# The skip mixing of a spectral layer, on images instead of transposed pixels

## The chip, the cores and the metric

The kernel runs on one core of a Trainium2 chip. The metric is device time in microseconds, lower is better. The engines are called as the profile calls them: PE (matmul), PEld (weight load), DVE (vector), ACT (scalar), POOL (GpSimd) and SP, which here only issues transfers.

## The reference, cut to what matters

Two layers work on an array of 4 x 32 images of 128 x 128 numbers, in float32. Layer 1 (a pairwise attention and a mixture of experts) is untouched. Layer 0 is a Fourier layer with attention over the 32 images of a set; for every set b:

```
x   = group norm of the input (32 groups of 4 of the last axis), then instance norm -> xn
k, q = spectral convolutions of xn at half size;  v = xn * Vsw + spectral_conv(xn)    (32 heads)
p_attn = softmax over the 32 images of (q . k)
av  = p_attn @ v
p   = av * Psw + spectral_conv(av, Pcw)        # summed over heads
a   = inorm(p + x);  then two more Fourier layers on inorm(a)
```

What passes through `v` and `p` by the skip weights alone needs no Fourier transform: it is a 32 x 32 mixing of the images of the set, the same for every pixel. That mixing (with the identity for `+ x`) is what the change is about: for each pixel, 32 numbers in, 32 numbers out, on the group-normed input.

## The kernel before

Layer 0 is a loop over b in 0..3, written in plain program order; a planner (the framework's list scheduler) orders each engine's instructions by their place in the program and by the time at which it expects them to be ready, so later work, loads above all, can be placed ahead of earlier work that is not ready. Layer 1 has its order written out by hand and follows.

The image set is held as `xt`: the rows (first pixel axis) on the 128 partitions, then 32 images, then 128 columns. The columns fall into 32 groups of 4 for the group norm; `image_sums` computes for each group the mean `gm` and the inverse deviation `gr`, and `by_group`, which holds `gr` and minus `gm * gr` of the 32 groups on all partitions.

Inside the loop over b, the part around the change runs so:

- From the attention probabilities `ph` the kernel makes `cp`, the 32 x 32 mixing, on four blocks of 32 partitions (`cm`, `cd`, lines 651 to 657), and from it the block matrix `bd` (line 659): 128 x 128, with the 32 x 32 mixing four times on the diagonal.
- `skips(c0)` treats 16 columns. It turns them so that four columns times 32 images lie on partitions and the rows on the free axis: 16 matmuls with the identity into `pxt` (line 671). Four ACT instructions norm and move them to `xq` (line 681), with the scale and bias of their group. Four matmuls with `bd` (line 690) give `sk`, with the rows on partitions again, and one ACT copy (line 693) puts them into `q`. Eight calls treat all 128 columns.
- The calls are spread over a loop that does the Fourier part: `for x0 in range(0, KX, NK)`, five passes over slices of the modes (13, 13, 13, 13 and 12 rows of 33 modes). In each pass four tiles `xb` are loaded from the DRAM tile `xd` (line 706, two transfers of 214.5 KB to a tile, four buffers), copied to PSUM as `xw` by ACT (line 715), and multiplied with the weights `gb`: 16 products `u` to a pass, six by POOL (line 721) and ten by DVE (line 723), in six buffers. Each `u` goes through PE with the probabilities `pr` (line 726), in matmuls with 32 output columns, and is summed in `po`, which ACT copies into `rs` at the end of the pass (line 736). Two calls of `skips` are made in each of the first four passes, after the tiles i = 1 and i = 3.
- After the passes, `py` (line 746) transforms `rs` back, and `add_p` (line 759, DVE) adds the result onto `q`, group of eight images by group. `q` is then used by all that follows in this b, and the output of the layer is stored to `x1` from `xr`, which is `xt` in place (line 919).

At the end of a b, `gl` (buffer tag `y`, one buffer) is scaled by ACT (line 902) and added to `xr` by POOL (line 909); the images of b+1 are loaded as `x` (line 122), from SP and ACT. In PSUM, tag `a` holds `po` and `pxt`, tag `b` holds `sk` (two buffers each).

Of the kernel before, what the change touches and what calls it, by code (L numbers as in the profile page):

```python
# [7 lines left out]
F32 = mybir.dt.float32  # L8
AF = mybir.ActivationFunctionType
ALU = mybir.AluOpType  # L10
# [3 lines left out]
P = 128  # L14
B, T, H, C = 4, 32, 128, 128
# [3 lines left out]
GI = 8  # L19
# [56 lines left out]
NK = 13  # L76
# [28 lines left out]
def layer0(  # L105
    tc, x, kq_modes, kq_mirror, vcw, pcw, m0cw, m1cw, mcol0, heads, heads_row, small_row, by_p, inv_cols, dram, x1, first
):
    nc = tc.nc
# [7 lines left out]
    const, ps, images, values, modes = (p.__enter__() for p in pools + right)  # L116
# [32 lines left out]
    ident = const.tile([P, P], F32, name="ident")  # L149
# [125 lines left out]
    def image_sums(b, xt):  # L275


        rows8 = ps.tile([64, 4, C], F32, name="rows8", tag="wide")
        for g in GROUPS:
            xx2 = grp.tile([P, GI, C], F32, name="xx2", tag="pr", bufs=6)  # L280
            nc.scalar.activation(xx2, xt[:, g : g + GI], AF.Square)
            for h in range(2):
                m = g // 4 + h
                for k, src in enumerate((xt[:, 4 * m : 4 * m + 4], xx2[:, 4 * h : 4 * h + 4])):
                    nc.tensor.matmul(
                        rows8[32 * k : 32 * k + 32],
                        one_of_8[:, 7 - m : 39 - m],
                        src,
                        start=m == 0,
                        stop=m == 7,  # L290
                    )
        ev = grp.tile([64, 4, C], F32, name="ev", tag="v", bufs=3)
        nc.scalar.copy(ev, rows8)
        s12 = ps.tile([P, 2, 512], F32, name="s12", tag="wide")[:, :, :T]
        for j in range(4):
            for k in range(2):
                r = slice(32 * k, 32 * k + 8)
                nc.tensor.matmul(s12[:, k, j::4], ev[r, j], ident[r, r], start=True, stop=True)
        sv = small.tile([P, 2, T], F32, name="sv", tag="pk_sq")
        nc.vector.tensor_copy(sv, s12)  # L300

        tot = one("tot", 2)
        nc.vector.tensor_reduce(tot, sv, AX.X, ALU.add)
        mg = sums("mg", group, tot)
        gm = one("gm")
        nc.vector.tensor_copy(gm, mg[:, 0:1])
        gv = one("gv")
        nc.vector.tensor_mul(gv, gm, gm)
        nc.vector.tensor_tensor(gv, mg[:, 1:2], gv, ALU.subtract)
        gr, _ = inv_std("gn_r", gv, 1)  # L310
        gs = one("gs")
        nc.vector.tensor_mul(gs, gm, gr)

        both = small.tile([P, 2, 32], F32, name="both", tag="both")
        nc.vector.tensor_scalar(both[:, 0], of_group, gr, None, ALU.mult)
        nc.vector.tensor_scalar(both[:, 1], of_group, gs, -1.0, ALU.mult, ALU.mult)
        by_group = small.tile([P, 2, 32], F32, name="by_group", tag="by_group")
        nc.vector.tensor_copy(by_group, sums("bg", ones, both))
        n = 1 + 2 * KY
        colg = small.tile([P, 2, n], F32, name="colg", tag="colg")  # L320
        nc.vector.tensor_scalar(colg[:, 0], cols1[:, :n], gr, None, ALU.mult)
        nc.vector.tensor_scalar(colg[:, 1], cols2[:, :n], gr, None, ALU.mult)
        m128 = one("m128")
        nc.vector.tensor_scalar(m128, gm, 128.0, None, ALU.mult)

        gs128 = one("gs128")
        nc.vector.tensor_scalar(gs128, gs, 128.0, None, ALU.mult)
        gg = one("gg")
        nc.vector.tensor_mul(gg, gs, gs128)
        gr2 = one("gr2")  # L330
        nc.vector.tensor_mul(gr2, gr, gr)
        grs = one("grs")
        nc.vector.tensor_scalar(grs, gs, gr, -2.0, ALU.mult, ALU.mult)
        y12 = small.tile([P, 2, T], F32, name="y12", tag="pk")
        nc.vector.tensor_scalar(y12[:, 0], sv[:, 0], gr, gs128, ALU.mult, ALU.subtract)
        nc.vector.tensor_scalar(y12[:, 1], sv[:, 1], gr2, gg, ALU.mult, ALU.add)
        nc.vector.scalar_tensor_tensor(
            y12[:, 1], sv[:, 0], grs, y12[:, 1], ALU.mult, ALU.add
        )
        nc.vector.tensor_scalar(y12, y12, 1.0 / NPIX, None, ALU.mult)  # L340
        my = sums("my", ones, y12)
        ym, yv = per_image("ym"), per_image("yv")
        nc.vector.tensor_copy(ym, my[:, 0])
        nc.vector.tensor_mul(yv, ym, ym)
        nc.vector.tensor_tensor(yv, my[:, 1], yv, ALU.subtract)
        yr, _ = inv_std("n1_r", yv)
        ysc = scalars(ALU.mult, "n1_s", yr, par[:, N1W : N1W + 1])
        return by_group, colg, m128, ysc
# [286 lines left out]
    for b in range(B):  # L635
# [27 lines left out]
            ALU.mult,  # L663
        )
        q = big.tile([P, T, C], F32, name=f"q_{b}", tag="q")

        def skips(c0):
            px = ps.tile([P, 4, P], F32, name="pxt", tag="a")
            for k in range(4):
                for j in range(4):  # L670
                    nc.tensor.matmul(
                        px[32 * j : 32 * j + 32, k],
                        xt[:, :, c0 + 4 * k + j],
                        ident,
                        start=True,
                        stop=True,
                    )
            xq = grp.tile([P, 4, P], F32, name="xq", tag="v", bufs=3)
            for k in range(4):
                g = c0 // 4 + k  # L680
                nc.scalar.activation(
                    xq[:, k],
                    px[:, k],
                    AF.Identity,
                    bias=by_group[:, 1, g : g + 1],
                    scale=by_group[:, 0, g : g + 1],
                )
            sk = ps.tile([P, 16, T], F32, name="sk", tag="b")
            for k in range(4):
                nc.tensor.matmul(  # L690
                    sk[:, 4 * k : 4 * k + 4], xq[:, k], bd, start=True, stop=True
                )
            nc.scalar.copy(q[:, :, c0 : c0 + 16], sk.rearrange("w c t -> w t c"))

        rs = big.tile([P, KX, KY], F32, name=f"rs_{b}", tag="rs")
        at_c = 0
        for x0 in range(0, KX, NK):
            nk = min(NK, KX - x0)  # L700
            m = nk * KY
            po = ps.tile([P, NK * KY], F32, name="po", tag="a")[:, :m]
            for i in range(4):
                xb = late.tile([P, 2, NK * KY], F32, name="xb", tag="xb")[:, :, :m]
                for r in range(2):
                    nc.sync.dma_start(
                        out=xb[:, r],
                        in_=xd[8 * i : 8 * i + 8, r, x0 : x0 + nk]
                        .rearrange("s x y -> s (x y)")
                        .unsqueeze(1)  # L710
                        .to_broadcast([8, 16, m]),
                    )
                xw = ps.tile([P, 2, 512], F32, name="xw", tag="wide")[:, :, :m]
                for r in range(2):
                    nc.scalar.copy(xw[:, r], xb[:, r])
                for k in range(2):
                    for ri in range(2):
                        u = grp.tile([P, 2, NK * KY], F32, name="u", tag="pr", bufs=6)[:, :, :m]
                        gk = gb[:, k, ri, x0 * KY : x0 * KY + m].unsqueeze(1).to_broadcast([P, 2, m])
                        if (2 * k + ri + 4 * i) % 8 in (1, 4, 6):  # L720
                            nc.gpsimd.tensor_tensor(u, xb, gk, ALU.mult)  # L721
                        else:
                            nc.vector.tensor_tensor(u, xw, gk, ALU.mult)  # L723
                        for r in range(2):
                            j = 2 * ri + r
                            nc.tensor.matmul(  # L726
                                po[32 * j : 32 * j + 32],
                                pr[:, i, k],
                                u[:, r],
                                start=i == 0 and k == 0,  # L730
                                stop=i == 3 and k == 1,
                            )
                if i % 2 and at_c < C:
                    skips(at_c)
                    at_c += 16
            nc.scalar.copy(rs[:, x0 : x0 + nk].rearrange("p x y -> p (x y)"), po)
        if b + 1 == B:
            for p in reversed(right):
                p.__exit__(None, None, None)
# [807 lines left out]
```

## Time and profile before

| what | value |
|---|---|
| time, three runs | 3195.37, 3197.76, 3202.53 us; median 3197.76 |
| span of the profiled execution, first to last instruction | 3194.2 us |
| PE busy | 2961.2 us (93%) |
| DVE, ACT, POOL busy | 2318.6, 2324.8, 2135.8 us |
| `skips` at work (first line 726 to last copy to `rs`), b = 0 to 3 | 108 to 177, 365 to 436, 633 to 702, 888 to 957 us |
| granted PE clock, mean | 0.967 |
| HBM read, written | 68.16, 20.00 MB |

The profiled execution has no time of its own beside its span in what is recorded; the span lies 3.6 us below the median of the runs. A row of a group of instructions reads: line, engine, operation, output <- inputs, shapes, number, busy time and mean duration of one. fp32 matmuls appear as two records each, and some records can be missing. In the rows of a window, the first number is its length, then the busy time of each engine with the number of its instructions, the granted PE clock, the mean busy share of the 16 DMA engines and the GB/s moved. In the rows of the chain of waits, the columns are start, duration and what ran.

### The profile page before, as it was taken

To read this page: it belongs to the slowest core of one execution; us is meant where nothing else is said; L and a number is where in the kernel's file an instruction comes from. 1 tells how busy PE (TensorE), PEld (TensorE's weight loads), DVE (VectorE), ACT (ScalarE), POOL (GpSimd) and SP (SyncE) were. 2 spreads that over 40 slices of the span, in tenths; PEclk is the share of its full clock that TensorE was granted. 3 is DMA by queue.
4 is the path that set the end of the run, shared out by engine and by line. 5 is a ranking of instruction groups with operands and counts; after the bars stand their busy time and mean duration, and the time that the engine had idled before them with its cause. 6 is when DMAs were issued, how large, how long until landed. Compare 5 with 4: busy or idle time off the path is not lost.

```text
span 3194.2 us, 53401 instructions
## 1 busy us (share of the span) xinstructions
PE 2961.2 (93%) x19698; PEld 1556.6 (49%) x19698; DVE 2318.6 (73%) x5072; ACT 2324.8 (73%) x3205; POOL 2135.8 (67%) x1879
## 2 busy tenths in 40 slices
PE   7899899899898889999999999998999999999997
PEld 4377367458558744443344443444444444444443
DVE  6766767768787466777666868866778776777887
ACT  2435344354343489998999999998999999999992
POOL 2621641561461289878788797889878889888773
PEclk8899999899998799999999999999999999999998
DMA  6301310230140211010111010011010011101000
GB/s 138 116 11 30 101 44 4 64 106 1 36 125 1 57 31 30 8 31 7 30 37 24 14 24 14 8 39 30 22 30 8 14 37 24 37 1 31 14 14 14
DMA packets 151925, 112.57 MB, mean 35 GB/s; under 512 B 36750, under 2 KB 140273, under 8 KB 151057
## 3 DMA queue, kind: packets, MB, share of 16 engines
q1 hardware_dynamic: 135825, 103.40, 12.2%
q10 hardware_dynamic: 15840, 5.77, 0.8%
q8 instruction: 156, 2.56, 0.3%
q14 instruction: 104, 0.85, 0.1%
HBM read 68.16 MB, written 20.00 MB: 28 GB/s over the span
## 4 chain that ended last, share of the span: by engine, by line
PE 56%; POOL 12%; ACT 9%; DVE 7%; issue 6%; DMA 0%; POOLq 0%; DVEq 0%; ACTq 0%; SPq 0%
PE d L1349 18%; PE po L1368 10%; PE px L1255 6%; ACT r L1399 4%; PE n L1349 3%; POOL e L1408 3%; POOL e L1407 3%; PE po L726 3%; PE four L261 2%; PE pv L256 2%; PE px L247 2%; PE px L246 2%; ACT e L1415 2%; POOL kx L1014 2%; DVE r L1404 2%
## 5 line engine op out<-in xcount | busy, mean ns | idle before, releaser
L1404 DVE TENSOR_TENSOR r<-n,r 128x1024 f32<-128x1024 f32 (+1 forms) x1056 | 961.8, 952 | 479.2 <-PE n L1349 398.5
L1407 POOL TENSOR_TENSOR e<-r 128x512 f32<-128x512 f32 x528 | 674.1, 1277 | 269.9 <-DVE r L1404 269.1
L1399 ACT ACTIVATE r<-d 128x1024 f32<-128x1024 f32 (+1 forms) x1056 | 793.4, 803 | 71.5 <-PE n L1349 57.8
L1411 ACT ACTIVATE r<-r 128x1536 f32<-128x1536 f32 x528 | 783.5, 1484 | 16.7
L1408 POOL TENSOR_TENSOR e<-e,r 128x512 f32<-128x512 f32 x528 | 672.1, 1273 | 41.4
L1349 PE MATMUL d<-qe,ke 32*128 32x512 f32 (+3 forms) x2304 | 606.7, 603 | 39.7 <-ACT r L1399 36.4
L1368 PE MATMUL po<-e,kx 128*128 128x512 f32 (+3 forms) x1152 | 594.4, 605 | 17.4 <-POOL e L1420 17.4
L1349 PE MATMUL n<-qe,ke 32*128 32x512 f32 (+3 forms) x2304 | 606.2, 601 | 0.0
L1349 PE MATMUL n<-qf,kf 32*128 32x512 f32 (+3 forms) x2304 | 552.3, 554 | 0.0
L1349 PE MATMUL d<-qf,kf 32*128 32x512 f32 (+3 forms) x2304 | 550.8, 554 | 0.0
L1259 DVE SCALAR_TENSOR_TENSOR xc<-px,wgt,xc 128x128 f32<-128x128 f32 x1024 | 358.3, 350 | 43.1 <-PE px L1255 10.6
L1415 ACT ACTIVATE e<-e 128x512 f32<-128x512 f32 x528 | 325.8, 617 | 67.2 <-POOL e L1408 66.2
L1368 PEld LDWEIGHTS po<-e,kx 128*128 128x128 f32 x1152 | 175.4, 188 | 393.7 <-issue 307.7
L1349 PEld LDWEIGHTS d<-qe,ke 32*128 32x128 f32 x2304 | 176.9, 184 | 359.5 <-ACT r L1399 340.1
L721 POOL TENSOR_TENSOR u<-xb,gb 128x858 f32<-128x858 f32 (+1 forms) x120 | 233.1, 1969 | 126.7 <-PE po L726 108.3
L1349 PEld LDWEIGHTS d<-qf,kf 32*128 32x128 f32 x2304 | 220.5, 186 | 176.9 <-issue 164.2
L811 POOL TENSOR_TENSOR spec<-spec,part 128x264 f32<-128x264 f32 x64 | 55.4, 865 | 336.6 <-DVE part L808 174.8
L1255 PE MATMUL px<-we,x2t 128*128 128x512 f32 x512 | 265.8, 605 | 6.9 <-DVE xc L1259 5.8
L723 DVE TENSOR_TENSOR u<-xw,gb 128x858 f32<-128x858 f32 (+1 forms) x200 | 206.5, 1085 | 51.4 <-PE po L726 34.3
L1349 PEld LDWEIGHTS n<-qf,kf 32*128 32x128 f32 x2304 | 228.0, 185 | 18.6 <-issue 11.2
L726 PE MATMUL po<-u,pr 128*32 128x429 f32 (+1 forms) x1280 | 187.5, 537 | 20.5 <-POOL u L721 8.7
L1349 PEld LDWEIGHTS n<-qe,ke 32*128 32x128 f32 x2304 | 177.8, 183 | 9.3 <-DVE r L1404 0.9
(360 smaller groups left out, 4184.3 us busy)
## 6 DMA issues: line engine op xcount, KB each, us to landing
xb<-xd SPq DMA_DIRECT2D x128, 214.5 KB
xc<-x SPq DMA_DIRECT2D x29, 512.0 KB
x<-x SPq DMA_DIRECT2D x16, 512.0 KB
qf<-qe SPq DMA_DIRECT2D x64, 128.0 KB
out<-xc SPq DMA_DIRECT2D x15, 512.0 KB
xb<-xd SPq DMA_DIRECT2D x32, 198.0 KB
gb<-gd SPq DMA_DIRECT2D x4, 1056.0 KB
x<-in_x SPq DMA_DIRECT2D x8, 512.0 KB
```

The source lines that it names most:

```text
L721: nc.gpsimd.tensor_tensor(u, xb, gk, ALU.mult)
L726: nc.tensor.matmul(po[32 * j : 32 * j + 32], pr[:, i, k], u[:, r], start=i == 0 and k == 0, stop=i == 3 and k == 1,)
L1255: nc.tensor.matmul(px, x2t[:, k * P : (k + 1) * P], we[:, e0 : e0 + 4], start=True, stop=True)
L1259: nc.vector.scalar_tensor_tensor(xc[:, k], px[:, e], wgt[:, k, e0 + e : e0 + e + 1], xc[:, k], ALU.mult, ALU.add)
L1349: nc.tensor.matmul(o, k, q, start=turn == 0 or g > 0, stop=turn == 1 or g > 0)
L1368: nc.tensor.matmul(sums[c, h][:, q0 : q0 + c1 - c0], kx[:, jb], e[:, c0:c1], start=jb == 0, stop=is_last and q0 > 2 * P, skip_group_check= ...
L1399: nc.scalar.activation(r[:, g], d, AF.Ln, scale=1.0 / DSCALE)
L1404: nc.vector.tensor_tensor(r[:, g], part, r[:, g], ALU.mult)
L1407: nc.gpsimd.tensor_tensor(e, r[:, 1], r[:, 2], ALU.add)
L1408: nc.gpsimd.tensor_tensor(e, e, r[:, 0], ALU.add)
L1411: nc.scalar.activation(r, r, AF.Exp, scale=-1.0)
L1415: nc.scalar.activation(e, e, AF.Exp)
```

## The change

The mixing works on a second copy of the images in which a partition is (width piece j, image t): `xs`, 4 pieces x 32 images on partitions, 32 rows of pixels x 128 columns on the free axis. (The axis called w in the diff is the first pixel axis, which is the partition axis of `xt`.) `load_by_image` loads it from the input in four transfers of 512 KB, after the first pass. In this form `bd` is the stationary operand and a whole 128 x 512 piece (4 rows of pixels) is the moving one. A second product adds `bd` times minus the group mean, so `by_group` now holds `-gm` instead of `-gm * gr`, and DVE multiplies the sum with `gr` back into `xs`. Each piece is stored to a DRAM tile `qd` (256 KB, pieces of 2 KB), and after the third pass four transfers bring `qd` back as `q`, rows on partitions (512 KB each, pieces of 512 bytes). The eight calls of `skips` now stand after each of the four tiles of passes 2 and 3 (`x0` = 13 and 26). `xs` takes the buffer tag `y`.

```diff
-        nc.vector.tensor_scalar(both[:, 1], of_group, gs, -1.0, ALU.mult, ALU.mult)
+        nc.vector.tensor_scalar(both[:, 1], of_group, gm, -1.0, ALU.mult, ALU.mult)
...
-        def skips(c0):
-            px = ps.tile([P, 4, P], F32, name="pxt", tag="a")
-            for k in range(4):
-                for j in range(4):
-                    nc.tensor.matmul(
-                        px[32 * j : 32 * j + 32, k],
-                        xt[:, :, c0 + 4 * k + j],
-                        ident,
-                        start=True,
-                        stop=True,
-                    )
-            xq = grp.tile([P, 4, P], F32, name="xq", tag="v", bufs=3)
-            for k in range(4):
-                g = c0 // 4 + k
-                nc.scalar.activation(
-                    xq[:, k],
-                    px[:, k],
-                    AF.Identity,
-                    bias=by_group[:, 1, g : g + 1],
-                    scale=by_group[:, 0, g : g + 1],
+        rows_of_4 = "t (j w) c -> j t w c"
+        qd = dram.tile([T, H, C], F32, name=f"qd_{b}")
+        xs = big.tile([P, H // 4, C], F32, name=f"xs_{b}", tag="y")
+
+        def load_by_image():
+            for j in range(4):
+                nc.sync.dma_start(
+                    out=xs[32 * j : 32 * j + 32], in_=x[b, :, 32 * j : 32 * j + 32]
                 )
-            sk = ps.tile([P, 16, T], F32, name="sk", tag="b")
-            for k in range(4):
-                nc.tensor.matmul(
-                    sk[:, 4 * k : 4 * k + 4], xq[:, k], bd, start=True, stop=True
-                )
-            nc.scalar.copy(q[:, :, c0 : c0 + 16], sk.rearrange("w c t -> w t c"))
+
+        def skips(w0):
+
+            r = slice(w0, w0 + 4)
+            sk = ps.tile([P, 4, 32, 4], F32, name="sk", tag="b")
+
+            def over_pixels(t):
+                return t.unsqueeze(1).unsqueeze(3).to_broadcast([P, 4, 32, 4])
+
+            nc.tensor.matmul(sk, bd, xs[:, r], start=True, stop=False)
+            nc.tensor.matmul(sk, bd, over_pixels(by_group[:, 1]), start=False, stop=True)
+            nc.vector.tensor_tensor(
+                xs[:, r].rearrange("p w (g k) -> p w g k", k=4),
+                sk,
+                over_pixels(by_group[:, 0]),
+                ALU.mult,
+            )
+            nc.sync.dma_start(out=qd.rearrange(rows_of_4, j=4)[:, :, r], in_=xs[:, r])
...
-        at_c = 0
+        at_w = 0
...
-                if i % 2 and at_c < C:
-                    skips(at_c)
-                    at_c += 16
+                if x0 and at_w < H // 4:
+                    skips(at_w)
+                    at_w += 4
             nc.scalar.copy(rs[:, x0 : x0 + nk].rearrange("p x y -> p (x y)"), po)
+            if x0 == 0:
+                load_by_image()
+            if x0 == 2 * NK:
+                for g in GROUPS:
+                    nc.sync.dma_start(
+                        out=q[:, g : g + GI], in_=qd[g : g + GI].rearrange("t w c -> w t c")
+                    )
```

## The prediction, made before the changed kernel ran

> **What bounds the kernel now.** I read the page's table of busy times first (PE busy 93% of 3194.2 us, but no line of the changed code among its first rows), then the first and last start of the changed lines: `skips` runs in four stretches of 69 to 71 us, one per image set b, at 108-177, 365-436, 633-702 and 888-957 us. Only there can the change act, so the rest is read from those stretches. The starts of the copies into `rs` (line 736) cut each stretch into the five passes of the loop over `x0`:
>
> b=0: 13.6, 14.4, 14.3, 14.3, 11.5 us; b=1: 18.4, 12.4, 13.3, 14.4, 11.7; b=2: 18.1, 11.2, 13.3, 14.4, 11.6; b=3: 16.9, 11.9, 13.3, 14.4, 11.6.
>
> Two skips are traced into each of the first four passes and none into the fifth. Windows over passes 2 and 5 of b=0 (us, then busy time of PE, PEld, DVE, ACT, POOL, then clock, DMA share, GB/s):
>
> ```profile
> 121.46:135.83 14.37, 14.12 (x155) 6.93 (x151) 10.71 (x11) 8.72 (x20) 11.86 (x7) 1.00 0.37 125
> 164.50:176.50 12.00, 9.88 (x100) 3.41 (x92) 8.07 (x9) 7.10 (x14) 10.03 (x6) 1.00 0.07 25
> ```
>
> A pass with two skips is a PE pass: 14.12 of 14.37 us. In the fifth, with only the remains of the fourth's second skip in it, PE has slack and POOL decides: the last u's are four POOL instructions on end. The chain of waits shows what a skip is on PE (start, us, what):
>
> ```profile
> 411.32 0.71 PE sk L690 x4
> 412.03 0.85 PE po L726 x6
> 412.88 0.42 PE sk L690 x2
> 413.30 0.84 PE po L726 x2
> 414.14 0.42 PE sk L690 x2
> 414.56 1.69 PE po L726 x17
> 416.24 0.33 PE pxt L671 x3
> 416.57 0.28 PE po L726 x3
> 416.85 0.55 PE pxt L671 x19
> 417.39 0.09 PE po L726
> 417.49 0.27 PE pxt L671 x8
> 417.75 0.02 issue
> 417.78 0.47 ACT xq L681
> 418.25 0.04 issue
> ```
>
> Of these 6.98 us (half a pass), sk is 1.55, the transposes pxt 1.15, the hand-over to ACT and back 0.53, and po 3.75. So a skip takes 3.2 us of the chain, and spoils po: two po records alone take 0.84 us, where eight together take 0.80 (166.73 to 167.54).
>
> **What the Trainium skill says.** "TensorE: Matmul & The Clock Gate", Part 3 (packing small matmuls): matmuls with 32 output columns run beside each other in the array. The trace agrees: 17 po records, 523 ns each, in 1.69 us. The new products use all 128 columns and run alone. "FP8 and Floating Point Precision", TensorE Precision Notes: fp32 takes four passes. The trace shows two records to a matmul; a 128-column fp32 product of 512 has 0.95 to 0.96 us from start to start. "SBUF — State Buffer", Who interferes with whom: a DVE instruction with one SBUF input does not block POOL. The new multiply reads PSUM and SBUF, as L723 does; its POOL neighbours hold 1.88 us, which agrees.
>
> **The change, part by part.**
>
> *PE.* Removed per skip: 16 transposes, 4 products, 3.2 us of chain and the spoiled po. Added: two 128x512 products into one bank. Price from a timeline of layer 1:
>
> ```profile
> 1501.93 1.12 PE L1368 MATMUL po<-e,kx 128*128 128x512 f32 x2
> 1502.89 1.02 PE L1255 MATMUL px<-we,x2t 128*128 128x512 f32 x2
> 1503.84 0.70 PE L1349 MATMUL d<-qe,ke 32*128 32x512 f32 x2
> ```
>
> That is 0.96 each, 1.92 a skip. The second product reads its moving operand with zero steps (32 group values spread over 4 x 32 x 4), which no PE row shows: from 0.96 to twice that; I take 0.96, since the column count is the same.
>
> *DVE.* Added per skip: one multiply 128x512, PSUM times a spread SBUF operand. L653 has that form, 680 ns; L759 agrees (686). 0.69 taken. *ACT* loses 4 x 0.457 and 0.59 per skip, 2.4 us; it is no bound, but its in-order wait goes: at b=1 the copy of q waits 4.82 us for sk, with the xw copies of the next u's behind it, and DVE then stands 5.07 us.
>
> *Where the skips sit.* Eight per b as before, but four in each of passes 2 and 3, none in 1, 4, 5.
> - Passes 4 and 5: POOL's six u at 1.88 to 1.95 make 11.3 to 11.7; DVE's ten at 1.06 are 10.6; PE's 64 po records, 0.80 to 0.87 per eight, 6.4 to 7.0. I take 11.7, and 10.9 for the fifth (12 of 13 columns). Against 57.5 and 46.4 us in sum over b: -10.7 and -2.8.
> - Pass 1: POOL waits for po and then has four u left at b=1 (366.4 on, 8 us); DVE has cp and six u. Taken: 12.3, 13, 13 and 14.5 (at b=3 a 5.35 us wait for an xb landing remains on the chain) against 67.0: -14.2.
> - Passes 2 and 3: PE 7.0 + 4 x 1.92 = 14.7, DVE 10.6 + 4 x 0.69 = 13.4, POOL 11.3. PE bounds; nothing hides it. 8 x 14.7 = 117.6 against 104.2: +13.4. Ends: 13.4 (DVE, if PE packs po at 6.0) and 18 (below).
>
> *Transfers*, all on SP's queue, 16 more issues per b at about 0.57 us as for xb, 9 us on a queue that issues 40 xb in 70 us.
> - xs loads, 2 MB: their buffer is that of gl, whose last reader is POOL's L909 (over at 330.4, 592.5 and 849.5). SP then issues nothing until 354, 617, 874, and the DMA stands still:
>
> ```profile
> 330.40:354.30 23.90, 20.89 (x120) 7.44 (x121) 15.41 (x22) 4.79 (x9) 17.08 (x9) 0.93 0.00 1
> ```
>
> 2 MB at the 200 to 250 GB/s of busy stretches is 8 to 10 us. Each of the four loads spans 32 partitions; "SBUF — State Buffer", the section on the DMA port swizzle, gives such a transfer 8 of 16 ports and 189 GB/s, so 11 us as an estimate (no row of the trace before shows this shape). I take it at nothing, covered by 24 us, provided that the planner pulls the load up to there, as it pulls the first xb loads (296-316). At b=0 the load meets x(1) and xb at 82-100; up to 4 us late, and I take 0. If the cover at b>0 is gone, it competes with x(b+1) at 368-380, where the DMA is full.
> - Stores, 256 KB each: SP waits for DVE's multiply, with the xb loads queued behind; xb has four buffers, about a pass of lead. Nothing.
> - q back, 2 MB in 512-byte pieces, after pass 3 (about 150 at b=0); its first reader L759 starts at 188.5. 9 us of transfer under some 30 us: nothing. The next xb loads stand behind it, at a DMA share of 0.37.
>
> *Group mean.* The changed line of `both` costs what it did.
>
> Sum: -14.2 + 13.4 - 10.7 - 2.8 = -14.3 us. All four stretches are serial with what follows (py waits for rs, L759 for py's results), so the gain stays. It is made on the profiled execution's span, 3194.2; the median of the three times shown is 3197.76, 3.6 above it, and times differ by 7, so I take the gain off the median: 3183.5, said as 3184.
>
> **The rivals.**
> 1. *Slower: the crowded passes lock step.* PE takes a skip pair only in its place among po, DVE multiplies it only in its place among u, and u has six buffers. If half of each pair is not overlapped with u's, a pass becomes 4 x (2.65 + 0.69 + about 1.1) = 18. Then 8 x 18 - 104.2 = +39.8, less 27.7: +12, 3210. It decides from 16.5 us a pass ((104.2 + 27.7)/8). For it: DVE and POOL already wait 12.0 and 23.2 us for po in the stretch of b=0. Against: two queues of u smooth it, and sk has two banks. 0.18.
> 2. *No change that shows: data late.* The xs load stays behind x(b+1): some 6 us in each of three stretches, +18, 3202. Or hand-overs make a crowded pass 15.7: -6, 3191. 0.10.
> 3. *Better*: PE packs po and a pass is DVE's 13.4: -14.3 - 10.4 = -25, 3173. 0.12.
> 4. That the change doesn't do what it says: the mean enters as a second accumulated product and the scale afterwards, the same sum; I see no missing part.
>
> The likeliest (3184, from 3175 to 3190) has 0.60.
>
> **How the numbers follow.** A measurement of this kernel tells about 0.2%, 6.4 us, from none. Faster: 0.60 + 0.12 = 0.72; same 0.10; slower 0.18. Range 3166 (case 3 with the first pass at POOL's 11.5 everywhere) to 3206, short of rival 1's middle.
>
> **What would show it.** Right: passes of about 12.5, 14.7, 14.7, 11.7, 11 us; PE over 13.5 us busy in passes 2 and 3; chain of passes 4 and 5 through POOL u; xs issued before 354 at b=1; no wait of L759 for a DMA. Wrong: passes 2 and 3 over 16.5 us with DVE waiting for sk and PE for u; PE waiting for xs; the new multiply over 1 us; a second product longer than the first.

## The result, and the profile after

The changed kernel takes 3242.89 us (median; 3238.65 to 3246.08) against 3196.57 before, a ratio of 1.0153 with a 95% interval of 1.0130 to 1.0177. It is slower by 1.5%, where 14 us less had been forecast. The profiled span is 3242.9 us, so 48.7 us more.

The four stretches are cut into passes as in the prediction, here summed over the four image sets (us). "First po" is the time at which the first stretch starts, with the first matmul into `po`; "between" is the sum of the three stretches of other work between the sets, and "tail" all that follows the last pass, with all of layer 1.

| kernel | first po | pass 1 | 2 | 3 | 4 | 5 | passes in all | between | tail |
|---|---|---|---|---|---|---|---|---|---|
| before | 108.0 | 67.0 | 49.9 | 54.3 | 57.5 | 46.4 | 275.1 | 573.1 | 2238.0 |
| after | 118.5 | 58.0 | 57.6 | 65.2 | 63.0 | 75.6 | 319.5 | 572.9 | 2232.0 |

The passes lose 44.4 us and the start of the first one 10.5. The tail, which the change does not touch, gives 6 back; in all the kernels below it lies between 2230 and 2242, so a span can differ by some us for no reason in the passes.

Windows of the kernel after over pass 2 and pass 5 of b=0, in the columns of the two rows shown of before (length, busy time of PE, PEld, DVE, ACT, POOL, clock, DMA share, GB/s):

```profile
129.30:144.10 14.80, 14.80 (x79) 4.20 (x79) 13.03 (x15) 4.60 (x10) 12.21 (x8) 1.00 0.47 158
175.90:194.70 18.80, 10.09 (x64) 2.62 (x64) 9.03 (x10) 5.46 (x10) 10.14 (x6) 0.71 0.54 152
```

Pass 2 is as forecast: PE is busy without a gap, 14.80 us against the 14.7 of the sum. Pass 5 is not. No engine is busy for more than 10.14 of its 18.80 us, though it holds the same 64 po records as before. The granted clock is lower here (0.71), but PE, at 10.09 us, isn't what the pass waits for. Something outside the engines sets its length. The chain of waits at b=1 names it (start, us, what):

```profile
424.71 10.04 DMA xb<-xd
...
435.38 11.70 DMA qd<-xs
...
447.15 0.37 SPq L738
...
449.74 1.57 SPq L738
...
451.42 1.70 SPq L703
...
453.15 5.90 DMA xb<-xd
```

Where the chain of before ran through PE and POOL, this one runs for 34 us, but for one ACT copy of 0.5 us, through transfers and SP's issues: an xb on its way for 10.04 us, then the last store of a piece (11.70 us), on which SP waits before the first load of q (L738), then the four loads of q, and only then the next xb issue (L703) and 5.90 us until it lands. Those who wait for the xb loads in the whole kernel are, before and after (us, times; one wait of 28.9 us makes up nearly all of the first entry of before):

```profile
  ACT xw L715: 29.3, 2
  POOL u L721: 7.8, 2
```

```profile
  ACT xw L712: 166.2, 85
  POOL u L718: 67.3, 24
```

SP's own timeline shows how the xb loads come to be late. These are four rows from pass 3 of b=0 (start, us spent on issuing, line, transfer):

```profile
147.26 0.99 SPq L692 DMA_DIRECT2D qd<-xs  x1
148.55 3.14 SPq L703 DMA_DIRECT2D xb<-xd  x2
151.78 0.94 SPq L692 DMA_DIRECT2D qd<-xs  x1
152.83 3.41 SPq L703 DMA_DIRECT2D xb<-xd  x2
```

In these rows SP goes from one issue to the next almost without a pause; the issue itself has become long, 3.14 us for two loads where the median of before was 0.57 for one. One store and one tile together take about 4.5 us, and a pass of 14.4 us needs a tile every 3.6. All this at a mean DMA share of 0.40 to 0.43 in that stretch.

### The profile page after: what moved, and what is told of

It is laid out like the page before. It is cut to its first block, busy times and chain, and to the rows that moved or that the text cites. A ratio compares the mean times of both kernels' runs of the same rounds, so it can differ in the third digit from the quotient of the medians.

```text
span 3242.9 us, 51061 instructions
## 1 busy us (share of the span) xinstructions
PE 2955.5 (91%) x18546; PEld 1496.5 (46%) x18546; DVE 2323.4 (72%) x5104; ACT 2260.4 (70%) x3045; POOL 2121.1 (65%) x1879
## 4 chain that ended last, share of the span: by engine, by line
PE 54%; POOL 12%; ACT 8%; DVE 7%; issue 6%; DMA 3%; SPq 1%; POOLq 0%; DVEq 0%; ACTq 0%
PE d L1353 18%; PE po L1372 10%; PE px L1259 6%; ACT r L1403 4%; PE n L1353 3%; POOL e L1412 3%; DMA xb<-xd 3%; POOL e L1411 3%; PE four L261 2%; PE pv L256 2%; PE px L246 2%; PE px L247 2%; ACT e L1419 2%; POOL kx L1018 1%; DVE r L1408 1%
## 5 line engine op out<-in xcount | busy, mean ns | idle before, releaser
L1415 ACT ACTIVATE r<-r 128x1536 f32<-128x1536 f32 x528 | 783.6, 1484 | 16.8
L1263 DVE SCALAR_TENSOR_TENSOR xc<-px,wgt,xc 128x128 f32<-128x128 f32 x1024 | 358.1, 350 | 41.6 <-PE px L1259 10.5
L718 POOL TENSOR_TENSOR u<-xb,gb 128x858 f32<-128x858 f32 (+1 forms) x120 | 220.9, 1859 | 191.0 <-PE po L723 114.0
L712 ACT COPY xw<-xb 128x429 f32<-128x429 f32 (+1 forms) x160 | 82.2, 515 | 324.8 <-DMA xb<-xd 166.2
L720 DVE TENSOR_TENSOR u<-xw,gb 128x858 f32<-128x858 f32 (+1 forms) x200 | 198.4, 1030 | 87.2 <-ACT xw L712 70.4
```

What stands on the lines that cost most here:

```text
L1263: nc.vector.scalar_tensor_tensor(xc[:, k], px[:, e], wgt[:, k, e0 + e : e0 + e + 1], xc[:, k], ALU.mult, ALU.add)
L1415: nc.scalar.activation(r, r, AF.Exp, scale=-1.0)
```

## The theories and the experiments

**Theory E, the engines.** The records of the packets show that a store of a piece (128 packets of 2048 bytes, 84 ns each) mostly has up to four packets in flight, so it seems to be carried by four of the sixteen DMA engines, 32 x 84 ns = 2.7 us each. The two loads of an xb tile (1716 bytes, 72 ns) have about eight in flight: 2 x 16 x 72 ns = 2.3 us on each of eight engines. If the four are among the eight, they need 5.0 us for a tile and a store. The Trainium skill, "DMA: Bandwidth & Descriptors", states the rule in the section on why a DMA increments its semaphore by 16 and not by 1: the number of engines is the largest up to 16 that divides the slowest dimension of both sides, and the lowest-numbered ones are used. By this the four are among the eight. The store is written with the slowest dimension j = 4, the xb load with 8 images. The counts of four and eight agree with the packets in the trace; which of the sixteen they are it doesn't record. The prediction didn't apply the rule.

**Theory O, the order.** SP's queue puts four loads of q, the first of which waits for the last store, ahead of the last six xb loads of the stage. The stores may be harmless by themselves.

**The rival to both** (Theory P in the expectations): the crowded passes 2 and 3, that is PE, DVE and their buffers (rival 1 of the prediction).

### The store's engines, alone, in the kernel before

Two kernels made from the one before, each with two extra stores of `xq` in every call of `skips`; they differ only in the layout of the DRAM tile, whose slowest dimension is 4 in the first and 128 in the second.

```diff
+        dd = dram.tile([2, T, H, C], F32, name=f"dd_{b}")         # first kernel
+        dd = dram.tile([2, P, T, C], F32, name=f"dd_{b}")         # second kernel
...
+            for s in range(2):
+                nc.sync.dma_start(out=dd[s].rearrange("t (j w) c -> j t w c", j=4)[:, :, r], in_=xq)   # first
+                nc.sync.dma_start(out=dd[s, :, r], in_=xq)                                             # second
```

First kernel (slowest dimension 4):

> The kernel before with nothing taken out: each of its skips (two in each of passes 1 to 4) also stores xq twice (256 KB each, not read by anything) to a DRAM tile laid out as in the change, so that the slowest dimension is 4. Theory E: engines shared by xb and the stores need 4 x 1.15 + 2 x 2.7 = 10.0 us in the 7.2 us of half a pass: with eight skips to a set, some 22 us less a lead of about 5 us to a set, so 50 to 80 us slower than before, 3245 to 3275. Theory O: SP has 16 more issues to a set at 0.55 us that wait for ACT; 0 to 20 us slower, and the same as its twin with 128 rows.

Second kernel (128):

> The twin of the other kernel with extra stores: same stores, same bytes, same place in SP's queue, but the DRAM tile has 128 rows, so the slowest dimension is 128. Theory E: a store takes 0.7 us of each of 16 engines, the shared ones need 6.0 us in 7.2: 0 to 10 us slower than before, 3195 to 3206. Theory O: as slow as the twin within 8 us.

Measured: 3265.99 us, ratio 1.0231 (1.0212 to 1.0249), for the first; 3194.51, ratio 1.0012 (1.0000 to 1.0024), for the second. The passes are 347.2 and 274.9 us in all, against 275.1 before. The bytes, the size of the packets and the order on SP's queue are the same; the layout, and with it the number of engines, differs. Those who wait for the xb loads, first kernel, then second:

```profile
  ACT xw L719: 97.3, 54
  POOL u L725: 58.5, 20
```

```profile
  ACT xw L719: 6.2, 9
  POOL u L725: 5.1, 3
```

So a store with the slowest dimension 4 delays xb, and one with 128 costs next to nothing: 0.1% in time, nothing in the passes. The packets of xb (1716 bytes) show that the two share engines: in passes 2 to 4 of the first kernel they are exactly four in flight for 38% of the time, against 2% before and 4% in the second kernel, as they would be if the stores hold up four of xb's eight engines. Theory E holds for the store alone.

### The change with the store on all engines

```diff
-        qd = dram.tile([T, H, C], F32, name=f"qd_{b}")
+        qd = dram.tile([P, H // 4, C], F32, name=f"qd_{b}")
...
-            nc.sync.dma_start(out=qd.rearrange(rows_of_4, j=4)[:, :, r], in_=xs[:, r])
+            nc.sync.dma_start(out=qd[:, r], in_=xs[:, r])
...
-                for g in GROUPS:
-                    nc.sync.dma_start(
-                        out=q[:, g : g + GI], in_=qd[g : g + GI].rearrange("t w c -> w t c")
-                    )
+                for j in range(4):
+                    g = slice(32 * j, 32 * j + 32)
+                    nc.sync.dma_start(out=q[g], in_=qd[g].rearrange("t w c -> w t c"))
```

> The changed kernel with the DRAM tile laid out as 128 rows (width piece, image) instead of images x rows, so that a store's slowest dimension is 128 and not 4; q comes back in four transfers by width piece instead of by image group. Theory E (engines): the stores of the change run on four of the 16 DMA engines, the xb loads on eight, and the four engines that serve both need 2.7 us for a store and 2.3 us for the two xb loads of a tile, 5.0 us where a pass has 3.6. With the store over all engines that falls to about 3.0. Then passes 3 and 4 go from 65.2 and 63.0 us (sums over the four sets) to about 59 and 47, the q loads find the stores landed, and the whole is 25 to 40 us faster than the changed kernel: 3203 to 3218. Theory O (order): the loss comes from the stores and q loads standing in SP's queue ahead of the xb loads, whatever engines they use: within 8 us of 3243. Theory P (crowding on PE and DVE): also within 8 us of 3243, since PE's and DVE's work is the same.

Measured: 3220.3 us, ratio 1.0091 (1.0067 to 1.0114), just short of what Theory E expected; passes 58.9, 57.0, 56.8, 42.6 and 79.9. Pass 4 falls from 63.0 to 42.6, 10.65 each: with xb on time it is what the prediction said (11.7) or better. But pass 5 stays at 19.1 to 21.1 each. SP's timeline of this kernel and the window of pass 5 at b=0:

```profile
159.13 5.38 SPq L738 DMA_DIRECT2D q<-qd  x4
164.62 6.35 SPq L702 DMA_DIRECT2D xb<-xd  x6
```

```profile
165.90:185.80 19.90, 8.95 (x64) 2.12 (x60) 6.83 (x8) 5.48 (x9) 9.97 (x6) 0.74 0.56 116
```

The q loads come sooner, since the stores have landed sooner, and still stand ahead of six xb loads; in pass 5 ACT waits some 11 us for xb, 8.1 of them in one piece. About half of the loss is left, and it lies where Theory O puts it. The edit also changes the shape of the q loads: each now spans 32 partitions instead of 128, and the four together take 12 to 13 us, where in the change they took 8 to 9.

### The loads of q, traced later

```diff
-            if x0 == 2 * NK:
+            if x0 == 4 * NK:
                 for g in GROUPS:
```

> The changed kernel with the q loads traced after the fifth pass instead of after the third; the store is as in the change. The planner then puts the q loads between the xb loads of the fifth pass instead of ahead of six of them. Theory O: the fifth pass (18.8 us against 11.6 before) loses its 7 us wait for xb: 20 to 29 us faster than the changed kernel, 3214 to 3223. Theory E: the first of the q loads still waits for the slow stores in the same queue, passes 3 and 4 stay at 16 us; a gain of 5 to 15 us at most, 3228 to 3238. Theory P: no change, 3243.

Measured: 3244.48, ratio 1.0159 (1.0136 to 1.0182), no gain, which neither Theory E nor Theory O expected. It is the time named for Theory P, but doesn't speak for it: pass 5 fell by 15.8 us to 59.8 and pass 4 grew by 13.5 to 76.5, though no skips are traced into either. SP's timeline shows the q loads between the last xb loads, as the expectation had it, at 168.3, 170.1, 172.4 and 177.2 us. The first of them still stands ahead of the last six xb loads, and SP again waited 6.8 us for the stores in front of it. So the wait moved from pass 5 to pass 4: the later place in the program didn't put the q loads behind the xb loads, and this edit can't settle Theory O. The next kernels force the place.

### The loads of q behind the last xb load

Two kernels: the change itself, and the change with the store on all engines, each with the q loads tied behind the last xb issue (`held` is that issue).

```diff
+            if x0 == 4 * NK:
+                with tc.issue_after(held["xb"].ins):
```

The change with this edit alone:

> The change itself, its store layout included, with one edit: its four q loads are traced after pass 5 and issued behind the last xb load. Bookkeeping of the lowest four engines (worked out after the earlier run with two skips a pass in this layout, whose passes 2 to 5 are 50.0 us a set): the xb of four tiles are there when pass 2 begins, so 12 tiles x 2.3 us + 8 stores x 2.7 us = 49.2 us a set, against 65.4 in the change, where SP also stands some 7 us for the last stores and 8 us of q loads run ahead of the last xb. Theory (order of q is most of the loss, the store's engines little once xb has its place): passes 2 to 5 about 50 to 52 us a set, 54 to 60 us less, add_p at most a few us later: about 3185 to 3192. Rival (the store's engines are most of it): passes 2 to 5 stay over 57, and the span over 3210.

With the store on all engines as well:

> The store layout of the earlier run (row-major by images and width pieces), and the four q loads issued on SP's queue behind the last xb load of the stage. Theory E (few DMA engines for the store, and the q loads ahead of the last xb loads; nothing else): pass 4 stays at 10.6 us, pass 5 falls from 19.9 to about 11, so the stages lose some 33 us against the first store-layout kernel and the span is about 3181, 10 to 15 us below the kernel before; add_p, first used some 12 us after the stage, waits at most a few us for q (13 us of transfer). Rival (q's transfer only moves its wait): add_p waits for q what pass 5 gains, and the span stays at about 3205 to 3214. Rival (crowding of DVE and PE is the loss): pass 5 stays over 15 us with no DMA wait in it.

Measured: 3217.86, ratio 1.0080 (1.0056 to 1.0105), for the first, and 3188.33, ratio 0.9980 (0.9971 to 0.9989), for the second. With the kernels above this makes a square (median time; passes in all):

| | q ahead of the last xb | q behind it |
|---|---|---|
| store on four engines | 3242.89; 319.5 (the change) | 3217.86; 289.6 |
| store on sixteen | 3220.30; 295.2 | 3188.33; 257.7 |

Alone, the store's mend takes 22.6 us off the time and 24.3 off the passes, and the order's mend 25.0 and 29.9. Both together take off 54.6 and 61.8. These are two causes of about one size, and without both mends the change doesn't come below the kernel before. The 7 us by which both together exceed the sum are no more than the interval of one ratio (some 7.5 us each way); the slower q loads of the mended store, which cost pass 5 some 4 us (79.9 against 75.6) as long as they stand ahead of xb, would explain a part of it.

By its numbers the rival of the first kernel's expectation held, narrowly: passes 2 to 5 fell from 65.4 to 57.7 us a set, where it said over 57, and the span is 3214.0, where it said over 3210. That the store's engines are most of the loss is more than the square shows. The account of 49.2 us on the lowest four engines came out too small, and the packets show why. At b=0 the stores' packets run from 132.8 to 170.4 us, 12 us into pass 4. In these 37.6 us they take 22.2 us of each of four engines, and those of xb 21.3 us of each of eight, as an estimate that spreads them evenly: more than there is on the engines that serve both. The last xb landed 51.7 us after the start of pass 2 (50 to 54 in the four sets), near the 49.2; but the work on it, 6.0 us, comes after that, and the account had left it out.

The second kernel came out as its expectation's Theory E had it: pass 5 is about 11 us and the profiled span 3181.9, though the median of its 14 runs lies 6 us above that. It shows the passes with the data on time, at b=0 passes 2, 4 and 5:

```profile
128.98:143.76 14.78, 14.78 (x79) 4.18 (x80) 13.01 (x15) 4.58 (x9) 12.20 (x8) 1.00 0.58 197
158.59:169.25 10.66, 8.19 (x64) 1.79 (x64) 10.66 (x12) 4.51 (x10) 10.66 (x7) 1.00 0.49 166
169.25:180.11 10.86, 7.74 (x64) 1.64 (x60) 6.61 (x8) 4.81 (x8) 9.87 (x6) 1.00 1.03 177
```

Pass 2 is PE's, pass 4 DVE's and POOL's, and pass 5 doesn't mind a DMA share of 1.03, because its xb are ahead of the q loads. The rival of the crowded passes falls as a cause of the loss: pass 2 of b=0 is 14.8 us in the slow kernel and in this one, and pass 3, with the same work, goes from 65.2 to 56.8 in sum.

add_p starts later here, 14.9 to 16.8 us after the stage where before it was 12.5 to 14.2. I took that for a wait for q, as the expectation said. It is not one, as DVE's timeline of this kernel at b=0 shows:

```profile
194.37 0.69 DVE L185 TENSOR_SCALAR v<-pv 66x512 f32<-66x512 f32 x1 [5.40 <-PE pv L257]
194.98 1.27 DVE L763 TENSOR_TENSOR q<-q,four 128x512 f32<-128x512 f32 x2
```

The last packet of q landed at 185.2; DVE stood 5.40 us for a copy that is placed ahead of the first add (L763). The order of DVE's instructions has changed, not the data. It costs little: "between" is 575.6 us against 573.1.

### The loads of xs at b=0

In the change the xs loads of the first set are issued ahead of the load of pr (the probabilities, which come back from the DRAM tile prd). From the issue of the store to prd until the first po it takes 11.9 us, before 4.6: SP waits 5.7 us for prd to land, where it was 1.5, and PE runs the first product of a skip, 2.1 us, ahead of the first po. These 7.3 us are most of the 10.5 by which the first po is late. The other 3 lie ahead of prd and are not put down to xs: the second kernel with extra stores, which has no xs, issues prd 4.4 us later than the kernel before.

Two kernels move the loads. The first adds this to the kernel with both mends:

```diff
+            with tc.issue_after(held["pr", 0].ins) if b == 0 else nullcontext():
```

> As the one before, and the four xs loads of the first image set are issued behind the load of pr. Theory E: the time from prd to the first po at b=0 falls from 12.0 to about 5 us as in the kernel before, and nothing else changes: 7 us less, about 3174. Rival (the xs loads are then late for the first skips, in pass 2 of b=0): pass 1 or 2 of b=0 grows by the same 7 us.

Measured: 3188.56, ratio 0.9978 (0.9966 to 0.9991), no gain, as the rival in the expectation said. From prd to the first po it is 4.6 us again (8.9 in the kernel without the edit), but pass 1 of b=0 grew from 10.8 to 18.2: PE waited up to 7.1 us for the second load of pr, which ACT issues at 108.67 beside xs. The second try issues xs on ACT's queue behind that load (in the kernel with two skips a pass, below):

```diff
-                    nc.sync.dma_start(
+                    (nc.sync if b else nc.scalar).dma_start(
```

> As the kernel with two skips in each of passes 2 to 5, but at b=0 the xs loads are issued on ACT's queue behind its pr load (k=1). Theory: the 16 KB packets of xs that run beside the second pr load hold up the first pass of b=0 (18.0 us against 13.5 before, PE waiting for pr up to 7 us); behind both pr loads they hold up nothing that is due: pass 1 of b=0 about 11 to 13 us, 5 to 7 us less in all, about 3166. Rival (2 MB landing in these 10 us are late for the first skip or hold up xb): pass 2 of b=0 grows by what pass 1 gains.

Measured: 3178.18, ratio 0.9945 (0.9926 to 0.9965), not separable from the kernel with xs on SP's queue behind pr. Pass 1 of b=0 fell to 10.8, and pass 2 grew to 22.1. PE's entry among the waits there:

```profile
PE sk L687 <- DMA xs<-in_x: 9.6, 1, 9.6
```

The 2 MB have now stood in three places, and a wait of 6 to 10 us stood in each: for prd, for pr, for xs itself. None of the three was an idle stretch.

### Two skips a pass

The next two kernels, too, have both mends and xs behind pr; they spread the skips over four passes.

```diff
-                if x0 and at_w < H // 4:
+                if x0 and i % 2 and at_w < H // 4:     # passes 2 to 5
+                if i % 2 and at_w < H // 4:            # passes 1 to 4, xs loaded ahead of pass 1
```

> As the one before, with two skips in each of passes 2 to 5 instead of four in passes 2 and 3. If the crowded passes cost what PE does (14.2 each measured, 10.6 without skips), two skips in a pass with POOL's slack cost about 11.5: eight crowded passes give back 8 x 2.7, eight empty ones take 8 x 0.9, so -14 us; but the q loads then follow the last skip at the end of the stage, and add_p, 12.5 us later, waits for up to 13 us of transfer. Expected from -14 to +10 against the one before. If passes 2 to 5 are over 13 us each, two skips a pass cost more than PE's share.

> As the one with xs behind pr, with two skips in each of passes 1 to 4. Passes 1 to 4 then hold PE 7.0 + 2 x 1.92 = 10.8, DVE 10.6 + 1.4 = 12.0, POOL 11.3: about 12 each. Against 58, 57, 57, 43 in sum over the sets: passes 2 and 3 -18, pass 4 +5, pass 1 +0 to +3: 10 to 13 us less, about 3162. If the crowded passes are not bound by PE there is no gain: about 3174. At b=0 the first skip may wait for xs in pass 1.

Measured: 3173.06, ratio 0.9935 (0.9909 to 0.9961), with skips in passes 2 to 5: passes 65.4, 45.5, 47.8, 45.6, 44.2, in all 248.4, 26.7 less than before; that is 15.5 us in time below the kernel with four skips in passes 2 and 3, where 14 had been expected at best. And 3180.55, ratio 0.9971 (0.9956 to 0.9986), with skips in passes 1 to 4: 257.1 in all, pass 2 52.8, and not the 10 to 13 us less that had been expected. Why passes 1 and 2 are longer there is open; the trace shows no wait for xs. The kernel with skips in passes 2 to 5 has the lowest median of all the kernels here. Its passes 3 and 5 at b=1:

```profile
394.33:405.40 11.07, 10.28 (x73) 3.03 (x74) 10.20 (x13) 4.59 (x10) 10.06 (x7) 1.00 0.57 185
416.79:427.83 11.04, 8.77 (x68) 2.14 (x68) 8.98 (x11) 4.89 (x8) 9.94 (x6) 1.00 0.34 121
```

In pass 3 PE, DVE and POOL are all between 10.1 and 10.3 of 11.1 us busy. Where the data are on time, such a pass is 0.4 to 0.8 us longer than the 10.65 without skips, so most of PE's 3.84 us for the pair lies beside POOL's and DVE's u's, where two pairs in one pass made PE the bound (14.0 to 14.8 us).

The same kernel with the change's store on four engines:

> As the kernel with two skips in each of passes 2 to 5, but with the change's own layout of the DRAM tile (slowest dimension 4) and its eight q loads. The order of the work is the same; only the engines that take the stores differ. Theory E: a tile of xb costs an engine of the lowest four 2.3 us, a store 2.7 us; with a store at every second tile that is 3.65 us a tile, 14.6 us a pass, against 11.1 to 11.4: passes 2 to 5 are 14 to 15 us each where the other kernel has about 11.3, some +45 us, 3210 to 3220. Rival (the stores hurt only because four of them crowd into one pass, on SP's queue): passes stay at about 11.3, and the span at 3170 to 3175.

(The q loads of that layout are four, not eight.) Measured: 3187.04, ratio 0.9968 (0.9953 to 0.9982); passes 2 to 5 are 199.9 us against 183.0, so +17 and not +45. The direction is Theory E's, the size little more than a third of it. The account had charged all sixteen tiles to these passes; without the four that are loaded before pass 2 it comes to 12 x 2.3 + 8 x 2.7 = 49.2 us a set, where 50.0 were measured. This was worked out afterwards, and that the xb buffers take up the rest isn't shown. Even with the four-engine stores this order comes out 0.3% below the kernel before.

### The loads of q in halves

```diff
-                    for j in range(4):
+                    for t in range(0, T, T // 2):
+                        for j in range(0, P, 32):
```

> As the kernel with two skips in each of passes 2 to 5, with each of its four q loads cut into two halves of 16 images, the first halves of all width pieces first. add_p begins with the first eight images, so it waits for half of the transfer only: from 15.0 to 16.8 us after the stage back to 12.5 to 14, some 8 to 10 us less, about 3162 in the span. Rival (add_p of the later images then waits for the second half, or eight issues are slower): the wait moves, and the span stays at 3168 to 3172.

Measured: 3181.53, ratio 0.9965 (0.9950 to 0.9981); add_p starts 14.9 to 17.5 us after the stage, as without the edit. No gain: it rested on the reading that add_p waits for q, which the DVE timeline above contradicts, and which this run contradicts too.

## Why the prediction was wrong, point by point

- **The step that failed** is "Transfers", for two of its three entries. "Stores ... Nothing": they delayed every xb load behind them, not mainly because SP waited for DVE's multiply, but because they share four engines with xb. "q back ... nothing. The next xb loads stand behind it, at a DMA share of 0.37": that q itself has cover was right (add_p starts 12.5 to 13.6 us after the stage, as before), but what stands behind it was seen and taken to be harmless. In the square above the first is worth 24 us of the passes by itself, the second 30, both together 62. Both were judged by the mean share over sixteen engines, and a mean of 0.37 before, or 0.47 after, can't show that four of them are full.
- **xs at b=0**, "up to 4 us late, and I take 0": 7.3 us, by way of the store of prd and the load of pr, which the prediction had not named as standing beside it and behind it. At b>0 it was right: the issues moved up to 352, 621 and 894 us and no one waited; the 2 MB took 10.6 us at b=3, near the 11 of the estimate.
- **PE, DVE**: right. Passes 2 and 3, 117.6 in the sum, are 122.8 in the change and 113.9 with the data on time. The new rows, the first product and the one with the spread operand, which had been bounded by 0.96 and twice that:

```profile
L684 PE MATMUL sk<-xs,bd x12: 592/592/697, 129.1 to 149.8; 128*128 128x512 f32 x12
L685 PE MATMUL sk<-by_group,bd x16: 592/593/697, 125.1 to 155.9; 128*128 128x512 f32 x16
```

  Both have the same record, and from start to start they take 0.96 and 0.95 us (from 129.07 on), so a moving operand read with zero steps costs no more here. The multiply L686 has a median of 680 ns, 0.69 taken.
- **Passes 4 and 5**, 46.8 and 43.6 in the sum: 63.0 and 75.6 in the change, 42.6 and 43.5 with both mends. **Pass 1**, 52.8: 58.0, mis-sized by 5; at b=1 it stayed at 18.2 against 18.5, so the skips had not been what made it long.
- **The sum**: with both mends the passes are 257.7 us, where the terms of the prediction make 260.8. The work on the engines was predicted; the transfers that feed it were not. Of the passes' -17.4 us the late first po takes 10.2 back and "between" 2.5: what remains, 5 us, fits the ratio of 0.998 (6 us).
- **The rivals**: that data come late was rival 2, but for xs, and sized at 5 us. Rival 1 had the sign, by luck: it put the loss into passes 2 and 3, by way of PE and DVE, and most of the loss came in pass 5 and from the transfers.

## What to carry to other kernels

Before a new transfer is put down as hidden, count the engines that carry it and those that carry its neighbours, from the packets in flight or from the slowest dimension of both sides, and price it per engine; here the mean share said nothing of that. Then ask what stands behind it on its queue: here a load that had to wait for a store held up all the loads after it on its queue for 6.8 us. And look in the queue's own timeline for the place that an instruction got; a later line in the program doesn't ensure it.

## What the runs showed of the hardware

- The time that SP spends on issuing a transfer is not fixed: for an xb load it has a median of 0.57 us before and 0.60 in the change, with single ones up to 3.3 and 5.0 us. In the two kernels with extra stores the medians are 0.93 us (slowest dimension 4) and 0.59 (128), for the same loads. So it grew with the stores that share four engines with xb, and the queue was then late for all that followed.
- 2 MB of q in 512-byte packets, with no xb load beside them, took 8.5 us at b=0 in loads that span 128 partitions (33 ns a packet on the mean; two skips a pass, four-engine stores) and 12.9 in loads that span 32 (51 ns; two skips a pass, stores on sixteen).
